# Attention with a mixture of experts on one core: eight multiplies on VectorE, expert adds and fetches later in the pair, outputs through SyncE

## The chip, the cores and the metric

The kernel runs on one core of a Trainium2 chip. A core has four engines that compute, each with an instruction queue of its own that it works off in order: TensorE (PE: matrix products, results go to the banks of PSUM), VectorE (DVE), ScalarE (ACT) and GpSimd (POOL). SyncE (SP) only issues transfers. Transfers (DMAs) are issued from the queues of SP, ACT or POOL. An instruction that has to wait, for another engine or for a transfer, holds everything behind it on its queue.

The metric is the time of one execution on the device in microseconds (us). The profile is of one execution, taken by the hardware profiler; its times are in us from its start.

## The reference, cut to what matters

The input x is 8 sequences of 512 tokens with 256 channels. The result is x plus attention plus a feed-forward layer, both of the normalised x.

```python
x = L0_attn_x                                   # (8, 512, 256)
xn = layernorm(x)
# attention: 16 heads of 64, keys and values through a latent of 128
latent = xn @ w_kv_down
k, v = split(latent @ w_kv_up); q = xn @ w_q
att = softmax(causal(q k^T / 8)); y = att v     # per head
attn = y @ w_out
# feed-forward: each token goes to its top 2 of 8 experts, and through shared weights
scores = sigmoid(xn @ gate_w.T + lb_bias); topw, topi = top_k(scores, 2)
topw = topw / (topw.sum(-1) + 1e-8)
for e in range(8):
    sel = (topi == e).any(-1); wmean = mean of topw over the tokens of e
    out = out + where(sel, mlp_e(xn) * wmean, 0)
out = out + shared_mlp(xn)
return x + attn + out
```

All of it is in float32.

## The kernel before, in words

**Pairs.** The work is laid out over 64 pairs of heads, m = 8 b + p for sequence b and pair p (line 813). For a pair, `scores` makes the products of q and k in four row blocks on TensorE; VectorE adds the mask and takes the minimum (L662), ScalarE takes the exponential and its sums (L669), VectorE transposes the result in blocks of 32 into the tile `blk` (`transposed`, L682 and L689). `moved` (L701) brings `blk` to `pt` with 16 transfers of 80 KB, so that keys lie on the partitions; in most pairs GpSimd issues 5 of them and SP 11. `inverse_sums` takes the reciprocal of the sums (L718), transposes it (L721), and sends it to a row in DRAM (GpSimd's queue, L723). `spread_sums` loads that row, broadcast over partitions, as `rb` (SP's queue, L731). Two pairs later (LAG = 2) `weighted` multiplies v and `pt` on TensorE into the PSUM bank `ps_y` (L744), ScalarE copies it to the tile `yT` (L756) and GpSimd multiplies `yT` by `rb` (L757). With `by_vector`, which only the last two pairs use, VectorE makes one product of `ps_y` and `rb` (L754).

**Projection.** Two to three pairs after a sequence's last head pair, `project` multiplies all its `yT` and the shared experts' hidden values with the output weights (`ps_o`, L118), ScalarE copies the result (L780), and `add_projection` adds it to the sums `acc_d` in DRAM with an accumulating transfer from GpSimd's queue (L786). `acc_d` began as a copy of x.

**Experts.** After the router, each token's normalised row is scattered to two slots in DRAM (`xg_d`, sorted by expert) with indirect transfers of 128 rows from GpSimd (`scatter`, L478, two for each of 32 tiles, and 14 for empty slots). This fills pairs S0 = 14 to 21. In these pairs GpSimd issues one `pt` transfer instead of five and ScalarE up to five. From pair E0 = BLOCK0 = 22 on, 39 tiles of 256 slots pass through the experts. For tile t: `expert_fetch` gathers the expert's weights (GpSimd, L517) and loads the rows `xg` (SP, L524); `expert_turn` transposes them on TensorE (`ps_x`) and copies their token numbers (`to`, GpSimd, L544); `expert_hidden` and `expert_down` make the products, and ScalarE writes `ye` (L569); `expert_add` adds `ye` to the rows of `acc_d`, with an indirect accumulating transfer of 128 rows from GpSimd (L576), two for each tile. Since any of these may touch any row of `acc_d`, each of them waits until the write to `acc_d` before it has landed.

**Order of the work.** All engines' queues are in the order in which the program is written out. `put(m, place, f)` enters a step in the plan of pair m (L808), and each pair's steps are issued by rising place; steps of one place in the order of entry. Up to pair 21 a pair has two halves (places from 0 and from 1), each with a group of scores; `moved` and `inverse_sums` for a pair are issued in the next pair, and `weighted` stands at place 1.4. From pair 22 on a pair has one block of scores. There the multiplication `weighted` of two pairs before comes first, and `inverse_sums` and `moved` of the pair itself are issued ahead of the first step whose place is above HALF:

```python
EARLY, HALF = 0.3, 0.65
...
if place > HALF and chunks:
    while chunks:
        transposed(*chunks.pop(0))
    inverse_sums(*pairs[m])
    moved(*pairs[m], 8 if m >= END else 5)
f(*a)
```

`put_half(h, place, f)` enters a step in half h, that is pair h // 2 at h % 2 + place. With it, tile t has its own half h (L925), from 49 on in steps of one or two. Its fetch stands five halves before, its two adds two and three halves after. So the places of fetches are 0.5 and 1.5, and those of adds 0.45 and 1.45. `rb` of the pair before is loaded at 0.34, the projection's steps stand at 0.75 and 1.7.

**The end.** From pair END = 59 on `bring_out` copies the finished sums of seven sequences from `acc_d` to the output (L792, from ScalarE's queue), one per half, places 0.7 and 1.7. The last sequence's sums are loaded, added to its projection on VectorE (L775) and stored by SP.

Of the kernel before, what the change touches and what calls it, by code (L numbers as in the profile page):

```python
# [33 lines left out]
F32 = mybir.dt.float32  # L34
# [7 lines left out]
P = 128  # L42
# [7 lines left out]
def kernel(  # L50
# [17 lines left out]
    nc = tc.nc  # L68

    B, T, C = x.shape  # L70
# [18 lines left out]
    NU = SLOTS // P  # L89
# [21 lines left out]
    def bank(shape, name):  # L111

        return psum.tile(shape, F32, tag="w", name=name)

    def product(out, lhsT, rhs, start, stop):

        for j in range(2):
            nc.tensor.matmul(  # L118
                out[ts(j, D)], lhsT[:, ts(j, D)], rhs, start=start, stop=stop
            )  # L120

    xf = x.rearrange("b t c -> (b t) c")
    outf = out.rearrange("b t c -> (b t) c")
# [99 lines left out]
    acc_d = dram.tile([NT_ALL, C], F32, name="acc_d")  # L223
# [337 lines left out]
    def expert_down(t):  # L561
        w = fetched[t][0]
        ps = bank([P, NU, C], "ps_ed")
        for u in range(NU):
            product(
                ps[:, u, :], hidden[t][:, ts(u, P)], w[:, ds(WD, C)], start=True, stop=True
            )
        y = ep.tile([P, NU, C], F32, bufs=3, name="ye")
        nc.scalar.mul(y, ps, coef[:, t : t + 1])  # L569
        results[t] = y  # L570

# [122 lines left out]
    def moved(b, p, by_pool, by_act=0):  # L694


        pt = ptp.tile([P, NB, 2, NBLK, QB], F32, name="pt")

        def begin(by, k):
            a, kb = divmod(k, NB)  # L700
            by.dma_start(pt[ts(kb, QB), a], blks[b, p][ts(a, QB), kb])  # L701

        left = []
        for k in range(NB * NB):
            if k * by_pool % 16 < by_pool:
                begin(nc.gpsimd, k)
            elif k % 3 == 1 and len(left) < by_act:
                left.append(k)
            else:
                begin(nc.sync, k)  # L710
        pts[b, p] = pt
        return lambda: [begin(nc.scalar, k) for k in left]

    def inverse_sums(b, p):


        ri, riT = ris[p % len(ris)]
        nc.vector.reciprocal(  # L718
            ri[:, : 2 * NQ], rss[b, p].rearrange("p j i -> p (j i)")
        )  # L720
        nc.vector.transpose(riT, ri)  # L721
        row = rowp.tile([NB, QB, QB], F32, name="row")
        nc.gpsimd.dma_start(row.rearrange("a x q -> (a x) q"), riT)  # L723
        rows[b, p] = row
# [64 lines left out]
        )  # L789

    def bring_out(b):
        nc.scalar.dma_start(outf[ts(b, T), :], acc_d[ts(b, T), :])  # L792

    def bring_back():
        nc.sync.dma_start(
# [8 lines left out]
    S0 = 14  # L804
# [3 lines left out]
    def put(m, place, f, *a):  # L808
        if place >= 2:
            m, place = m + 1, place - 2  # L810
        plan.setdefault(m, []).append((place, len(plan[m]) if m in plan else 0, f, a))

    pairs = [(b, p) for b in range(B) for p in range(NPAIR)]
    LAG = 2
    products = {}
    for m, (b, p) in enumerate(pairs):
        if m + 1 < len(pairs):
            put(m, 0.22, keys, *pairs[m + 1])
            put(m, 0.24, queries, *pairs[m + 1])
        if m < BLOCK0 - 1:  # L820
            put(m + 1, 0.32, inverse_sums, b, p)
        put(m + 1, 1.32 if m + 1 < BLOCK0 else 0.34, spread_sums, b, p)
        if m + LAG < BLOCK0:
            put(m + LAG, 1.4, weighted, b, p)
        else:
            products[m + LAG] = (b, p)
        put(m, 1.25 if m < BLOCK0 else 0.26, values, b, p * 2 // VH, p % 2)
    for b in range(B):
        m = b * NPAIR
# [39 lines left out]
    def put_half(h, place, f, *a):  # L869
        put(h // 2, h % 2 + place, f, *a)  # L870
# [5 lines left out]
    for b in range(1, B):  # L876
        h = (b - 1) * LNH // 2
# [41 lines left out]
        xouts = ep.tile([P, NQ, C], F32, name="xout")  # L919

    END = len(pairs) - 5
    put(E0, 0.1, begin_experts)
    first, n_halves = 2 * E0 + 5, 2 * (END - E0) - 7
    for t in range(NET):
        h = first + t * n_halves // NET  # L925
        put_half(h - 5, 0.5, expert_fetch, t)
        put(h // 2, -1, expert_turn, t)
        put(h // 2, (0.23, 0.67)[h % 2], expert_hidden, t)
        put_half(h + 1, 0.15, expert_down, t)
        for u in range(NU):  # L930
            put_half(h + 2 + u, 0.45, expert_add, t, u)
    for b in range(B - 1):
        put_half(2 * END + b, 0.7, bring_out, b)
    put_half(2 * END + B - 1, 0.7, bring_back)

# [3 lines left out]
    for m in range(len(pairs) + 1):  # L939
# [48 lines left out]
        for place, _, f, a in todo + [(2, 0, lambda: None, ())]:  # L988
# [3 lines left out]
# [6 lines that stand above are left out]
# [59 lines left out]
```

## Time and profile before

| | |
|---|---|
| time, median of 3 runs | 936.95 us (930.66 to 940.15) |
| profiled execution, own time | 937.93 us |
| its span, first to last instruction | 936.2 us |
| mean granted TensorE clock | 0.98 |
| TensorE busy | 888.7 us (95%) |
| GpSimd busy | 602.7 us (64%) |
| VectorE busy | 580.5 us (62%) |
| ScalarE busy | 506.7 us (54%) |
| scatters L478 | 62.6 us for the 64 of token rows, 979 ns each |
| multiplies of yT L757 on GpSimd | 88.2 us, 62 |
| indirect adds L576 | 127.5 us, 78, 1635 ns each |

How to read it: a group's row names line, engine, operation and the tiles it writes and reads; "L757 POOL TENSOR_TENSOR yT<-yT,rb 128x512" is GpSimd multiplying `yT` by `rb`. Busy time is the time in which instructions compute, or in which GpSimd makes up the descriptors of a transfer. Waiting and SP's or ACT's issuing of transfers are not busy. For a transfer, the duration at its line is that of its issue, and the data lands later. In a list of waits, the engine and the line that waited are named first, then what ended the wait; where it waited for several things, the name is that of the last one. "PEclk" is the share of TensorE's full clock that was granted.

### The profile page before, as it was taken

To read this page: it belongs to the slowest core of one execution; us is meant where nothing else is said; L and a number is where in the kernel's file an instruction comes from. 1 tells how busy PE (TensorE), PEld (TensorE's weight loads), DVE (VectorE), ACT (ScalarE), POOL (GpSimd) and SP (SyncE) were. 2 spreads that over 40 slices of the span, in tenths; PEclk is the share of its full clock that TensorE was granted. 3 is DMA by queue.
4 is the path that set the end of the run, shared out by engine and by line. 5 is a ranking of instruction groups with operands and counts; after the bars stand their busy time and mean duration, and the time that the engine had idled before them with its cause. 6 is when DMAs were issued, how large, how long until landed. Compare 5 with 4: busy or idle time off the path is not lost. (4 is left out here: it accounts for less than half of the span.)

```text
span 936.2 us, 20693 instructions
## 1 busy us (share of the span) xinstructions
PE 888.7 (95%) x6564; PEld 471.2 (50%) x6564; DVE 580.5 (62%) x2049; ACT 506.7 (54%) x1520; POOL 602.7 (64%) x840
## 2 busy tenths in 40 slices
PE   7897999988699899999999999899999999989898
PEld 3343555333354455645555545565556654546446
DVE  3887766996345785376753767535676356763761
ACT  3665565445335475465754666545576456753550
POOL 2795782388888855648676566675667656767460
PEclk9899999999999999999999999999999999999999
DMA  7578787468768898778888788887788687866782
GB/s 242 137 210 215 210 251 191 105 184 274 244 200 230 259 239 206 172 164 195 204 184 195 175 191 196 189 199 166 176 197 216 154 196 167 209 144 160 201 249 76
DMA packets 125195, 181.87 MB, mean 194 GB/s; under 512 B 24704, under 2 KB 88448, under 8 KB 124848
## 3 DMA queue, kind: packets, MB, share of 16 engines
q1 hardware_dynamic: 87760, 104.06, 39.8%
q0 software_dynamic: 34624, 69.28, 32.7%
q10 hardware_dynamic: 2704, 7.22, 2.6%
q8 instruction: 53, 0.87, 0.4%
q14 instruction: 54, 0.44, 0.2%
HBM read 66.45 MB, written 41.14 MB: 115 GB/s over the span
## 5 line engine op out<-in xcount | busy, mean ns | idle before, releaser
L662 DVE CUSTOM_DVE_ANT_0 ps_s<-ps_s,mask 128x128 f32<-128x128 f32 (+3 forms) x512 | 238.9, 519 | 189.2 <-PE ps_s L655 186.2
L669 ACT ACTIVATE pr<-ps_s,mn 128x128 f32<-128x128 f32 (+3 forms) x512 | 269.0, 537 | 125.0 <-DVE mn L662 94.5
L682 DVE STREAM_TRANSPOSE blk<-pr 128x384 f32<-128x384 f32 (+2 forms) x512 | 207.1, 446 | 33.4 <-ACT pr L669 16.3
L576 POOL DMA_INDIRECT acc_d<-ye,to x78 | 127.5, 1635 | 133.3 <-DMA acc_d<-ye,to 61.8
L701 POOL DMA_DIRECT2D pt<-blk x303 | 164.2, 692 | 42.9 <-DVE riT L721 22.3
L744 PE MATMUL ps_y<-pt,v 128*64 128x512 f32 (+3 forms) x1024 | 159.0, 454 | 21.6 <-DMA rb<-row 11.0
L655 PE MATMUL ps_s<-k,q 64*128 64x128 f32 (+3 forms) x1024 | 169.5, 449 | 9.5 <-ACT pr L669 4.5
L655 PEld LDWEIGHTS ps_s<-k,q 64*128 64x128 f32 x1024 | 92.3, 188 | 71.7 <-issue 36.7
L118 PE MATMUL ps_o<-wo_sb,yT 128*64 128x256 f32 x1024 | 121.1, 380 | 6.3 <-POOL yT L757 6.3
L744 PEld LDWEIGHTS ps_y<-pt,v 128*64 128x64 f32 x1024 | 75.0, 141 | 103.1 <-issue 73.7
L118 PE MATMUL ps_q<-xnT,wq_sb 128*64 128x512 f32 x512 | 122.9, 601 | 0.0
L757 POOL TENSOR_TENSOR yT<-yT,rb 128x512 f32<-128x512 f32 x62 | 88.2, 1423 | 50.7 <-ACT yT L756 32.9
L669 ACT ACTIVATION_READ_ACCUMULATOR pr<-ps_s,mn 128x1 f32 x512 | 108.3, 212 | 0.0
L118 PEld LDWEIGHTS ps_o<-wo_sb,yT 128*64 128x64 f32 x1024 | 77.3, 137 | 40.5 <-POOL yT L757 6.8
L118 PE MATMUL ps_e<-xgT,w 128*64 128x256 f32 x624 | 74.1, 379 | 0.0
L662 DVE DVE_READ_ACCUMULATOR2_ANT mn<- 128x1 f32 x512 | 72.5, 142 | 0.0
L118 PEld LDWEIGHTS ps_q<-xnT,wq_sb 128*64 128x64 f32 x512 | 38.3, 140 | 67.7 <-issue 60.0
L478 POOL DMA_INDIRECT xg_d<-xn,at_i x64 | 62.6, 979 | 13.3 <-issue 11.8
L118 PE MATMUL ps_k<-lat,wkv_sb 128*64 128x512 f32 x256 | 69.7, 622 | 1.0 <-ACT lat L600 1.0
L118 PE MATMUL ps_v<-wkv_sb,lat 128*64 128x256 f32 x512 | 68.4, 387 | 0.0
L780 ACT COPY po<-ps_o 128x256 f32<-128x256 f32 x28 | 10.4, 372 | 106.6 <-PE ps_o L118 106.6
L756 ACT COPY yT<-ps_y 128x512 f32<-128x512 f32 x62 | 36.6, 590 | 44.8 <-PE ps_y L744 43.4
(141 smaller groups left out, 959.6 us busy)
## 6 DMA issues: line engine op xcount, KB each, us to landing
pt<-blk SPq DMA_DIRECT2D x681, 80.0 KB
pt<-blk POOLq DMA_DIRECT2D x303, 80.0 KB
rb<-row SPq DMA_DIRECT2D x128, 128.0 KB
xg<-xg_d SPq DMA_DIRECT2D x39, 272.0 KB
acc_d<-in_x_dram SPq DMA_DIRECT2D x8, 512.0 KB
xin<-in_x_dram SPq DMA_DIRECT2D x7, 512.0 KB
xnT_d<-lnT SPq DMA_DIRECT2D x7, 512.0 KB
xnT<-xnT_d SPq DMA_DIRECT2D x7, 512.0 KB
```

The source lines that it names most:

```text
L118: nc.tensor.matmul(out[ts(j, D)], lhsT[:, ts(j, D)], rhs, start=start, stop=stop)
L478: ins = nc.gpsimd.indirect_dma_start(out=xg_d[:, :], out_offset=bass.IndirectOffsetOnAxis(ap=at, axis=0), in_=rows, in_offset=None,)
L576: nc.gpsimd.indirect_dma_start(out=acc_d[:, :], out_offset=bass.IndirectOffsetOnAxis(ap=turned[t][1][:, u : u + 1], axis=0), in_=results[t ...
L655: nc.tensor.matmul(pss[j][:, ds(at, n)], q[ts(j, D), ts(i, P)], k[ts(j, D), :n], start=True, stop=True,)
L662: nc.vector.tensor_tensor_reduce(out=pss[j][:, ds(at, n)], in0=pss[j][:, ds(at, n)], in1=mask[:, T - n :], scale=1.0, scalar=NO_MIN, op0=A ...
L669: nc.scalar.activation(o, s, AF.Exp, bias=mn, scale=-1.0, accum_out=rs[:, j, i : i + 1])
L682: nc.vector.transpose(blk[:, :, j, i : i + (nr - 1) * (NQ - 1) + 1 : NQ - 1, :].rearrange("p b c q -> p c b q"), pr[:, j, : nr * P].rearra ...
L701: by.dma_start(pt[ts(kb, QB), a], blks[b, p][ts(a, QB), kb])
L744: nc.tensor.matmul(ps[ts(j, D), :, c:, :], vs[b, h // VH][:, c, ts(h % VH, D)], pts[b, p][:, :, j, at : at + NQ - c, :], start=(c == 0), s ...
L756: nc.scalar.copy(y, ps)
L757: nc.gpsimd.tensor_tensor(y, y, rb, ALU.mult)
L780: nc.scalar.copy(pos[b][:, tt % 2, :], ps)
```

## The change

Three parts.

In pairs 14 to 21, while rows are scattered, `weighted` is called with `by_vector`: VectorE multiplies `ps_y` by `rb` into `yT`, in place of ScalarE's copy and GpSimd's multiply.

From pair 22 on the places of fetches and adds become 0.7 in a pair's first half and 1.45 in its second. 0.7 is above HALF, so `inverse_sums` and `moved` of the pair are issued ahead of them. `expert_fetch` moves as a whole: its gather of weights on GpSimd's queue and its load of rows on SP's. The tile `ye` has five buffers, not three.

`bring_out` issues from SP's queue.

```diff
-        y = ep.tile([P, NU, C], F32, bufs=3, name="ye")
+        y = ep.tile([P, NU, C], F32, bufs=5, name="ye")
...
     def bring_out(b):
-        nc.scalar.dma_start(outf[ts(b, T), :], acc_d[ts(b, T), :])
+        nc.sync.dma_start(outf[ts(b, T), :], acc_d[ts(b, T), :])
...
         if m + LAG < BLOCK0:
-            put(m + LAG, 1.4, weighted, b, p)
+            put(m + LAG, 1.4, weighted, b, p, S0 <= m + LAG)
...
+    def behind(h):
+
+        return h // 2, (0.7, 1.45)[h % 2]
+
     put(E0, 0.1, begin_experts)
     first, n_halves = 2 * E0 + 5, 2 * (END - E0) - 7
     for t in range(NET):
         h = first + t * n_halves // NET
-        put_half(h - 5, 0.5, expert_fetch, t)
+        put(*behind(h - 5), expert_fetch, t)
         put(h // 2, -1, expert_turn, t)
         put(h // 2, (0.23, 0.67)[h % 2], expert_hidden, t)
         put_half(h + 1, 0.15, expert_down, t)
         for u in range(NU):
-            put_half(h + 2 + u, 0.45, expert_add, t, u)
+            put(*behind(h + 2 + u), expert_add, t, u)
```

## The prediction

> **What bounds the kernel now.** I began with the page: engines' shares and the 40 slices.
>
> ```profile
> PE 888.7 (95%) x6564; PEld 471.2 (50%) x6564; DVE 580.5 (62%) x2049; ACT 506.7 (54%) x1520; POOL 602.7 (64%) x840
> ...
> PE   7897999988699899999999999899999999989898
> ```
>
> TensorE looks like the bound, GpSimd (POOL) like an engine with a third to spare. That average misleads, so I took busy times of stretches: 187-323 is about the scatter stage (pairs 14 to 21), 415-860 the expert stage with its adds, and two short ones lie around the worst hole. The columns are busy times of TensorE, its weight loads, VectorE, ScalarE and GpSimd, then the granted clock.
>
> ```profile
> core 0: us, PE busy (x) PEld busy (x) DVE busy (x) ACT busy (x) POOL busy (x), PEclk, DMA share, GB/s
> 187.00:323.00 136.00, 119.32 (x706) 55.26 (x706) 83.15 (x299) 64.59 (x200) 115.41 (x197) 0.95 0.79 232
> 243.00:256.00 13.00, 6.67 (x51) 3.35 (x51) 2.83 (x10) 4.04 (x13) 11.25 (x21) 0.96 0.74 230
> 256.00:269.00 13.00, 13.00 (x84) 6.78 (x84) 4.06 (x17) 3.97 (x12) 11.30 (x21) 0.77 0.74 215
> 415.00:860.00 445.00, 437.69 (x3360) 241.85 (x3358) 272.58 (x940) 260.15 (x774) 294.58 (x353) 0.99 0.79 185
> ```
>
> In the scatter stage TensorE is idle 16.7 us and its clock is below full. The timeline there (start, duration, idle before and who ended it) shows the one long wait:
>
> ```profile
> 254.61 1.28 POOL L757 TENSOR_TENSOR yT<-yT,rb 128x512 f32<-128x512 f32 x1
> ...
> 255.94 1.12 PE L118 MATMUL ps_o<-wo_sb,yT 128*64 128x256 f32 x4 [6.33 <-POOL yT L757]
> ```
>
> The product of that multiply had been copied out of PSUM by ScalarE at 243.9. It stood 10.7 us in GpSimd's queue behind scatters.
>
> In the expert stage I asked what GpSimd itself waits for (total, times, longest):
>
> ```profile
> POOL acc_d L576 <- DMA acc_d<-ye,to: 55.4, 24, 5.1
> POOL acc_d L576 <- issue: 35.6, 32, 4.5
> POOL acc_d L786 <- DMA acc_d<-ye,to: 12.1, 6, 3.1
> POOL acc_d L576 <- ACT xgT L540: 10.4, 3, 6.3
> ```
>
> All rows of that answer that stand before an accumulation into acc_d (L576, L786) add up to 136.7 us, the others to 11.8. With 294.6 busy this makes 443.1 of the 445 us: **GpSimd's queue is full in this stage.** The names "issue" and "ACT xgT" are the last event, not the cause: the adds' operand (ye) was written 10 to 20 us earlier. Each add waits for the landing of the previous write to acc_d. Two neighbours show the price:
>
> ```profile
> 589.44 1.69 POOL L576 DMA_INDIRECT acc_d<-ye,to  x1 [0.30 <-issue]
> 596.25 1.58 POOL L576 DMA_INDIRECT acc_d<-ye,to  x1 [5.13 <-DMA acc_d<-ye,to]
> ...
> 601.88 1.21 POOL L723 DMA_DIRECT2D row<-riT  x1
> ```
>
> The thirteen pairs of accumulations with nothing between them idle 2.88 to 6.29 us, 4.1 on average. The last line is pair 41's row of inverse sums, ready since 589: GpSimd is 13 us late. What that does to TensorE stands in the chain of waits:
>
> ```profile
> 824.15 1.62 DMA acc_d<-ye,to
> 825.77 2.86 issue
> ...
> 829.83 1.17 POOL row L723
> 831.00 1.47 POOL pt L701 x3
> 832.47 2.55 DMA pt<-blk
> ...
> 835.36 4.02 PE ps_y L744 x16
> ```
>
> TensorE lost 3.8 us in the slices of this piece. In 415-860 it lost 7.3 in all.
>
> **The change, part by part,** against the profiled execution: span 936.2, own time 937.9, 1.0 above the median of 936.95.
>
> *Multiply on VectorE, in pairs 14 to 21 (for the heads of pairs 12 to 19).* Gone: 8 GpSimd multiplies at 1.28 plus 0.17 gap, 11.6 us of a queue busy 115 of 136, and 8 ScalarE copies at 0.59, 4.7 us. New: 8 VectorE multiplies out of PSUM at 0.69 (the L754 row has two, at the tail), 5.5 us. The 6.33 us wait goes, since no product stands behind scatters any more. After it TensorE ran at 0.77 of its clock for 13 us: 3.0 us more. In 208-243 ScalarE is in steady work or issuing moves, and 0.59 less per pair may come through for three of them; I take 1.5. Sum: 10.8 us gained. Next late there is ScalarE itself, which issues five pt moves a pair and sat 29.3 us behind them in this stage, so I count no more. For the new wait: VectorE now stands at ps_y and at the rb load, and behind it are the next pair's minima (L662), which ScalarE's exponentials wait for. ps_y of pair 14 ends at 227.6, the minima before it ended at 225.7 and the transposes fill the time till then; the next minima began at 228.05 and then waited 2.36 us for TensorE. That wait covers 0.69, so I cost it at nothing; uncovered it is 5.5 us. The rb loads were issued 3 to 15 us before their ps_y, and come sooner when row stands behind less. Bounds of this part: 5 to 13 gained.
>
> *Adds and fetches behind row and pt.* The instructions are the same; what changes is what stands between two writes to acc_d. GpSimd's order in a pair was: index copy, multiply, add, fetch, row, five pt moves, add, fetch. It becomes: index copy, multiply, row, pt, add, fetch, add, fetch. Ahead of TensorE's needs come row and pt, so the wait shown in the chain is taken off that piece. But row and pt (0.6 + 2.5 us) no longer cover the landing of the pair's first add. I wrote out the plan for pairs 25 to 58: 86 accumulations, 85 intervals.
> Before: 13 with nothing between, 6 with a fetch (1.3 us), 12 with copy and multiply (1.65), 5 with a copy more (1.85), 15 with these and a fetch (2.98), 20 with row and pt (3.15), 14 others. At 4.1 us of idle time less what stands between, this leaves 53 + 17 + 29 + 11 + 17 + 19 + 3 = 149 us. The profile's own waits in 340-900 are 151, so the price holds.
> After: 25 with nothing, 19 with a fetch, 8 with row and pt, 8 with copy and multiply and the like, 25 covered. 102 + 53 + 8 + 15 = 178: **29 us more on a queue that is full.**
> Here a rule of the Trainium skill would turn the sum. "DMA: Bandwidth & Descriptors", Anatomy of one DMA, gives a DMA about 2.0 us fixed plus bytes by 436 GB/s, so 2.3 us for 128 KB (an estimate from the page). At 2.3 the adds' waits would be 47 before and 79 after; the queue would have 100 us of slack and 32 more would be hidden. The row says 4.1, and 149 against 151 confirms it. I follow the row.
> What of 29 reaches the end? GpSimd may fall behind until TensorE waits: row of pair 58 is 8.6 us late now; in pairs of 11.2 us TensorE stalls from about 11 to 12 (pair 56: 12.2 late, stalled 3.8), in longer pairs from about 16. So some 7 us is absorbed, and 22 remain. The stall comes at ps_y (row and pt late in short pairs, as reciprocal, row and everything wait for the former pair's adds) and at the projection, which needs the last pair's yT. Bounds: 0 if the landing gets as quick as the page says, 36 if nothing is absorbed and two or three stalls cost 3 us of clock each, as the hole at 250 did.
>
> *xg loads on SP* move behind the pt moves too. Later tiles have two or three pairs. The first tile has not: its load was issued at 322.9, and with eleven or twelve moves at 0.65 ahead it comes at about 330.6, while its transposes ran at 332.4. Landing takes 3 to 5.7 us here: 1 to 4 lost, I take 2. The buffers of ye (3 to 5) only keep ScalarE from waiting on late adds: 0.
>
> *Outputs through SP.* Seven issues of 0.5 to 0.6 us leave ScalarE and go behind pt of pairs 59 to 62 on SP, ahead of the next rb (868.69, 887.18, 897.82) and pt. SP needed 8.0 to 10.0 us for eight moves there, and ended 0.1 to 0.4 before rb, so two issues delay rb and the next pt by about 1.1. They also wait for the last adds, some 10 us later than now; pairs of 16.7 us hide most of that. ScalarE's exponentials gain the issues. "Issuing engines are not separate DMA queues" in the same page says that only issue time changes hands, as all run on the same 16 engines; by it this part is 0, by the SP rows 1.1 to 2.2 on the late chain. I take 1 lost, between a gain of 2 and a loss of 5.
>
> Sum: 937.9 - 10.8 + 22 + 2 + 1 = 952.1, and 951.1 by the median. I say 951.
>
> **The rivals.**
> *Faster: the queue catches up.* If landing falls to 3 us or less when adds follow adds (the shortest seen was 2.88 idle), the extra waits fit in the slack that this opens, and row and pt being first takes away the 7.3 us of stalls with 1.8 of clock. 937.9 - 10.8 - 9.1 + 3 - 1 = 920. For it speaks the chain; against it the mean of 4.1. It decides where the extra waits stay below the queue's slack. 0.18.
> *A draw.* Half of the extra wait shows (the measured landings go down to 3 in parts, lag absorbed early), 13 against 11: 938 to 940. 0.12.
> *Slower still.* SP waits at rb for late rows, pt and xg behind it come late, the transposes of the expert rows stall, and each stall brings a clock at 0.77: 22 becomes 40, so 969. 0.10.
> *Forecast:* 942 to 963, 0.60.
>
> **How the numbers follow.** About 1% tells no change for this kernel (its three runs span 930.7 to 940.2), so 927.6 to 946.3. Of the forecast's 0.60 a sixth lies below 946. Slower 0.50 + 0.10 = 0.60; same 0.10 + 0.12 + 0.01 = 0.23; faster 0.17. The range reaches from 926, above the heart of the faster case, to 968.
>
> **What would show it.** Right: no wait of ps_o for yT near 250, and clocks of 0.9 or more there; GpSimd's waits before L576 and L786 near 180 us, adds back to back; TensorE waiting 20 us or more at ps_y or ps_o in 415-870, for pt, row or yT; row still 10 to 15 us behind its reciprocal. Wrong: rows within 2 us of the reciprocal throughout, TensorE full in the expert stage. Then the price of a landing was mine to lose. If VectorE waits at L754 for rb by more than 5 us, the first part is wrong.

## The result, and the profile after

| | before | after |
|---|---|---|
| time, median of 20 runs each | 936.11 us (926.90 to 945.06) | 945.75 us (940.13 to 954.63) |
| after / before | | 1.0123, 95% interval 1.0093 to 1.0153 |
| profiled execution, own time | 937.93 us | 954.63 us |
| its span | 936.2 us | 952.9 us |

The medians are of all executions; the ratios, here and below, leave out those more than 1.5% above the fastest of their kernel.

The change costs 9.6 us by the medians, where 14 was forecast. The profiled execution of after is the longest of its runs, 8.9 us above their median; its 16.7 us of added span are therefore more than the change usually costs, and where the other 7 us lie isn't known, so the sizes below are rough. I place the difference with one event in each pair of heads, the start of VectorE's reciprocal (L718):

| from, to | before | after | difference | forecast |
|---|---|---|---|---|
| start to reciprocal of pair 13 | 202.1 | 202.9 | +0.8 | 0 |
| scatter stage, to pair 22 | 120.1 | 113.5 | -6.6 | -10.8 |
| expert stage, to pair 59 | 537.9 | 559.8 | +21.9 | +24 (adds 22, xg 2) |
| tail, to the end | 76.1 | 76.7 | +0.6 | +1 |

The page of after, engines' shares and TensorE's slices:

```profile
PE 894.5 (94%) x6564; PEld 470.4 (49%) x6564; DVE 585.2 (61%) x2057; ACT 502.4 (53%) x1512; POOL 590.2 (62%) x832
...
PE   8997999988998899999999998999969999989798
```

Again the shares say little: GpSimd is less busy than before, and it is GpSimd that costs the time. The windows of after, same stretches and columns as before:

```profile
187.00:323.00 136.00, 125.88 (x750) 56.71 (x748) 92.81 (x325) 64.80 (x205) 110.82 (x197) 0.96 0.82 241
243.00:256.00 13.00, 11.81 (x76) 5.54 (x76) 6.67 (x26) 5.38 (x17) 10.96 (x21) 1.00 0.87 264
256.00:269.00 13.00, 13.00 (x106) 7.16 (x104) 5.90 (x20) 6.35 (x20) 11.17 (x21) 1.00 0.89 269
415.00:860.00 445.00, 424.05 (x3236) 235.30 (x3234) 264.03 (x910) 252.46 (x748) 274.28 (x333) 0.98 0.75 179
```

The hole near 250 is gone (TensorE 11.81 of 13 us where it had 6.67), and the clock behind it is full where it was 0.77. In the expert stage TensorE is idle 20.95 us where it was 7.31. GpSimd's own waits there, in after (total, times, longest):

```profile
POOL acc_d L576 <- DMA acc_d<-ye,to: 72.6, 24, 6.0
POOL acc_d L576 <- ACT pr L669: 20.7, 5, 4.6
POOL acc_d L576 <- DMA pt<-blk: 17.2, 6, 5.3
```

From 340 us to about pair 62's reciprocal, all waits ahead of an accumulation add up to 181.2 us, against 151.1 before. The hand count of intervals gave 178 against 149. Accumulations with nothing between them are 25 in after, as counted, and 13 before; they idle 4.2 us on average, as before (4.1). GpSimd's timeline in after shows both kinds of neighbours:

```profile
463.03 1.60 POOL L576 DMA_INDIRECT acc_d<-ye,to  x1 [2.87 <-ACT xgT L540]
...
465.42 1.20 POOL L723 DMA_DIRECT2D row<-riT  x1
466.03 3.09 POOL L701 DMA_DIRECT2D pt<-blk  x5
470.06 1.68 POOL L576 DMA_INDIRECT acc_d<-ye,to  x1 [0.94 <-DMA acc_d<-ye,to]
476.27 1.60 POOL L576 DMA_INDIRECT acc_d<-ye,to  x1 [4.53 <-DMA acc_d<-ye,to]
```

The add at 470.06 has row and pt ahead of it and waits 0.94; the one at 476.27 follows an add directly and waits 4.53. The change makes more of the second kind. Rows fall further behind their reciprocals: 13.3 us on average in pairs 33 to 48, up to 18.8, against 8.1 before. TensorE's waits, first before and then after, from 320 us to the end:

```profile
PE ps_y L744 <- DMA pt<-blk: 3.8, 1, 3.8
PE ps_y L744 <- DMA rb<-row: 3.6, 2, 2.6
PE ps_y L744 <- ACT pr L669: 2.5, 1, 2.5
PE ps_y L744 <- DMA xg<-xg_d: 1.8, 1, 1.8
PE ps_y L744 <- DMA row<-riT: 1.3, 2, 0.8
```

```profile
PE ps_y L744 <- DMA pt<-blk: 13.8, 4, 7.4
PE ps_x L534 <- DMA xg<-xg_d: 6.6, 3, 4.5
PE ps_y L744 <- DMA rb<-row: 4.8, 1, 4.8
PE ps_y L744 <- ACT pr L669: 2.9, 3, 1.6
PE ps_e L118 <- DMA w<-wall_d,wrow_i: 2.2, 2, 1.6
PE ps_o L118 <- POOL yT L757: 0.5, 1, 0.5
```

These are 13.0 us before and 30.8 after. In the expert stage itself, without 3.9 and 4.8 us that lie in the tail (its waits for rb and row), they are 9.1 and 26.0. Of these 16.9 us more, 7.6 are at ps_y, 8.8 at the late fetches (xg and w) and 0.5 at ps_o. The other 5.0 of the 21.9 us are longer busy time for the same matmuls, and that goes with the clock: it was granted at half for 20.5 us of this stage, in three stretches around the long waits at 330, 714 and 838, where before had two of 3.4 us.

### The profile page after: what moved, and what is told of

It is laid out like the page before. It is cut to its first block, busy times and chain, and to the rows that moved or that the text cites. A ratio compares the mean times of both kernels' runs of the same rounds, so it can differ in the third digit from the quotient of the medians.

```text
span 952.9 us, 20647 instructions
## 1 busy us (share of the span) xinstructions
PE 894.5 (94%) x6564; PEld 470.4 (49%) x6564; DVE 585.2 (61%) x2057; ACT 502.4 (53%) x1512; POOL 590.2 (62%) x832
## 4 chain that ended last, share of the span: by engine, by line
PE 58%; DMA 21%; SPq 7%; DVE 5%; POOL 4%; issue 3%; ACT 2%; ACTq 0%; POOLq 0%; DVEq 0%
PE ps_o L118 13%; PE ps_y L744 10%; DMA pt<-blk 8%; PE ps_s L655 8%; PE ps_q L118 7%; SPq L701 5%; PE ps_e L118 5%; PE ps_k L118 4%; PE ps_gu L118 4%; DMA row<-riT 4%; PE ps_v L118 3%; DMA rb<-row 3%; DMA acc_d<-ye,to 2%; PE ps_ed L118 2%; DMA xg<-xg_d 2%
## 5 line engine op out<-in xcount | busy, mean ns | idle before, releaser
L701 POOL DMA_DIRECT2D pt<-blk x303 | 163.9, 695 | 38.8 <-DVE riT L721 10.4
L655 PE MATMUL ps_s<-k,q 64*128 64x128 f32 (+3 forms) x1024 | 172.1, 452 | 9.3 <-ACT pr L669 3.1
L757 POOL TENSOR_TENSOR yT<-yT,rb 128x512 f32<-128x512 f32 x54 | 79.3, 1469 | 45.8 <-ACT yT L756 29.1
L118 PEld LDWEIGHTS ps_o<-wo_sb,yT 128*64 128x64 f32 x1024 | 74.8, 137 | 37.0 <-issue 1.7
L723 POOL DMA_DIRECT2D row<-riT x64 | 49.5, 774 | 24.6 <-DVE riT L721 15.8
L756 ACT COPY yT<-ps_y 128x512 f32<-128x512 f32 x54 | 31.9, 590 | 58.5 <-PE ps_y L744 57.5
```

The lines of the kernel that those rows point to most:

```text
L118: nc.tensor.matmul(out[ts(j, D)], lhsT[:, ts(j, D)], rhs, start=start, stop=stop)
L655: nc.tensor.matmul(pss[j][:, ds(at, n)], q[ts(j, D), ts(i, P)], k[ts(j, D), :n], start=True, stop=True,)
L756: nc.scalar.copy(y, ps)
L757: nc.gpsimd.tensor_tensor(y, y, rb, ALU.mult)
```

## The experiments

They ran on two chips: the first four together on one, the other eight on a second, four at a time. The kernel before took 947.80, 955.71 and 954.55 us beside them, not 936, so every ratio below is to the kernel before on the same chip. Which chip the comparison above ran on isn't recorded; its two profiles are called the first pair below. There is no profile of the kernel before on the two chips: `e3_outputs`, which differs from it behind pair 59 only, stands in for it. The lengths of stages are from one profiled execution each.

### One part at a time

`e1_multiply`, the kernel before with the first part alone:

```diff
-            put(m + LAG, 1.4, weighted, b, p)
+            put(m + LAG, 1.4, weighted, b, p, S0 <= m + LAG)
```

> The first part alone: in pairs 14 to 21 VectorE multiplies yT, all else as before. Queue theory (the loss is in GpSimd's order of adds): 6 to 11 us faster than before, no wait of TensorE for yT near 250, VectorE's wait at L754 covered. Rival (VectorE standing at ps_y holds the minima and is what cost time): no gain or 3 to 6 us slower.

`e2_late`, the kernel before with `behind` for fetches and adds and with five `ye` buffers:

```diff
-        put_half(h - 5, 0.5, expert_fetch, t)
+        put(*behind(h - 5), expert_fetch, t)
...
-            put_half(h + 2 + u, 0.45, expert_add, t, u)
+            put(*behind(h + 2 + u), expert_add, t, u)
```

> The second part alone: fetches and adds behind row and pt, ye with five buffers, multiply and outputs as before. Queue theory: 16 to 22 us slower than before, waits in front of the accumulations on GpSimd about 180 us, row of inverse sums 10 to 18 us behind its reciprocal in pairs 41 to 58. Rival (the loss is in SP's queue at the end): within 3 us of before.

`e3_outputs`, the kernel before with the outputs on SP:

```diff
-        nc.scalar.dma_start(outf[ts(b, T), :], acc_d[ts(b, T), :])
+        nc.sync.dma_start(outf[ts(b, T), :], acc_d[ts(b, T), :])
```

> The third part alone: outputs through SP. Queue theory: within 2 us of before. Rival (outputs ahead of rb and pt on SP make the end late): 4 to 10 us slower, and the last four pairs longer by that.

`e4_multiply_outputs` has the edits of e1 and e3.

> First and third part without the late adds. Queue theory: 6 to 11 us faster than before, the same as the first part alone within 2 us. Rival (outputs on SP cost): 4 us or more slower than the first part alone.

| | median | ratio to before (95%) | scatter stage | expert stage | tail |
|---|---|---|---|---|---|
| e1_multiply | 969.95 | 1.0231 (1.0167 to 1.0295) | 164.3 | 533.1 | 74.3 |
| e2_late | 968.11 | 1.0243 (1.0183 to 1.0302) | 130.7 | 548.7 | 78.1 |
| e3_outputs | 943.88 | 0.9963 (0.9924 to 1.0003) | 131.7 | 538.1 | 72.8 |
| e4_multiply_outputs | 969.89 | 1.0240 (1.0178 to 1.0303) | 163.5 | 530.3 | 71.6 |

The late adds cost 20 us by the medians, as expected. Their profile is of the shortest execution, 7 us under its median, and shows 16 of them: 10.6 us in the expert stage and 5.3 in the tail, beside e3. The waits ahead of accumulations are 167 us there (180 was expected) against 142 in e3, rows 12 us late in pairs 41 to 58. The outputs alone gained 3.9 us by the medians, outside the 2 expected, but the interval reaches nothing, and e4 is as long as e1. The multiply is a plain miss: 22 us lost where 6 to 11 gained was expected, twice. The stage lengths put the loss where the multiply is: 164 us of scatter stage against 131 with GpSimd's multiply on the same chip. TensorE sat idle 46.5 us of it where it was 20.0, and its clock was 0.82, not 0.95. The waits of e1 from 203 to 366 us name it:

```profile
ACT pr L669 <- DVE mn L662: 40.1, 7, 9.9
DVE yT L754 <- remote: 30.7, 3, 10.7
...
PE ps_s L655 <- DVE yT L754: 20.3, 2, 10.3
```

VectorE stood three times for about 10 us at L754, and behind it ScalarE (no minima) and TensorE (no free bank). That is the standing which the prediction costed at nothing and put at 5.5 us uncovered. "remote" says that the view found no event of this core to end the wait.

### The adds: does the wait for the former write make the loss?

`e5_two_sums_late` is the changed kernel with the second add of each tile going to another tile in DRAM, so that two neighbours don't wait for each other. Half of the experts' results is thereby left out of the output. The second sum also begins as a copy of x: eight more transfers, 4.2 MB, most of them in the scatter stage.

```diff
-            out=acc_d[:, :],
+            out=(acc_d, acc2_d)[u][:, :],
```

> The changed kernel, but the second add of each tile goes to a second tensor in DRAM that also begins as a copy of x and never reaches the output (so half of the experts' adds are left out of the result). It takes away half of the waits for the landing of the write before, with the order of the queue kept. Queue theory: GpSimd catches up, row within 6 us of its reciprocal in most pairs of the expert stage, TensorE's stalls there under 5 us, and 920 to 932 in all. Rival (xg, rows and outputs late on SP): 940 or more, and TensorE still waits for pt and xg.

`e6_two_sums` has the same edit on e4, that is with the old order of adds and fetches; the same half is left out.

> The same second tensor (half of the experts' adds left out of the result) in the old order of fetches and adds, with the first and third part. Queue theory: when waiting for the landing is no longer the bound, order is worth little: 920 to 932, within 4 us of the same edit in the new order. Rival: 10 us or more faster than in the new order.

The other way to relieve GpSimd is to take its multiplies away in the expert stage too. `e7_late_all_vector` does it to the changed kernel, `e8_all_vector` to e4:

```diff
-            weighted(*products.pop(m))
+            weighted(*products.pop(m), True)
```

> The changed kernel, and VectorE multiplies yT in the expert stage too: 1.45 us a pair (about 50 in all) off GpSimd's queue, 0.69 a pair onto VectorE's. Queue theory: that is more than the 29 us that the new order put on it, so the stalls go: 918 to 932. Rival (GpSimd's work is not what counts, the landing chain of 86 adds alone is): 940 or more, rows still 10 us late.

> First and third part, adds in the old order, and VectorE multiplies yT in the expert stage too. Queue theory: GpSimd gets slack in the old order, 915 to 926, and the old order's stalls at 585, 700 and 830 go. Rival (VectorE standing at ps_y delays transposes and minima): slower than with the multiply in the scatter stage alone.

| | median | ratio to before (95%) | scatter stage | expert stage | row behind reciprocal, pairs 33 to 48 |
|---|---|---|---|---|---|
| e5_two_sums_late | 972.75 | 1.0160 (1.0091 to 1.0229) | 159.3 | 532.8 | 1.2 us |
| e6_two_sums | 964.78 | 1.0089 (1.0061 to 1.0118) | 165.5 | 526.8 | 1.3 us |
| e7_late_all_vector | 976.86 | 1.0208 (1.0140 to 1.0276) | 156.9 | 542.6 | 8.8 us |
| e8_all_vector | 976.16 | 1.0200 (1.0128 to 1.0273) | 171.5 | 530.3 | 8.0 us |

All four totals missed: 915 to 932 us was expected. All four carry VectorE's multiply in the scatter stage, and its loss on these chips hides in every total, so only the expert stage can be read. The groups of the page for the indirect adds, first of the changed kernel repeated on e5's chip (`e10_after_again`, below) and then of e5:

```profile
L576 POOL DMA_INDIRECT acc_d<-ye,to x78 | 126.7, 1625 | 164.6 <-DMA acc_d<-ye,to 88.9
```

```profile
L579 POOL DMA_INDIRECT acc_d<-ye,to x78 | 126.7, 1624 | 29.5 <-issue 21.1
```

With two sums the idle time ahead of the adds falls from 164.6 to 29.5 us, rows follow within 1.2 us on average, and the stage with late adds becomes 20 us shorter (553.0 in e10 to 532.8). The stage of e10 is no odd one: in e11, e12 and e13 below, which leave it as it is, it takes 549.7, 550.8 and 557.0. With the old order the second sum makes it 3.5 us shorter (e4 to e6, which ran on different chips). So the waits for the former write make some 17 us of what the late order costs, between 11 and 21 with these other stages and with e1's 533.1 for e4's. 6 us remain between the two orders without these waits (e6 to e5), and TensorE's waits in e5 show where (8.0 us in this stage, where under 5 was expected; the second row lies in the tail):

```profile
PE ps_x L537 <- DMA xg<-xg_d: 7.2, 2, 6.9
PE ps_y L747 <- DMA pt<-blk: 2.1, 1, 2.1
```

e6 has no wait for xg at all. It is the first tile's rows, loaded behind the pt moves: TensorE waited 4.5 us for them in after, 5.7 in e2, 6.9 here.

Taking the multiplies from GpSimd gave 7 to 14 us of this stage in the late order (550 to 557 in the four profiles, 542.6 in e7), and nothing in the old one (530.3 in e4 and e8, on different chips). Rows stayed 8 to 9 us behind in both. Some 50 us of multiplies became waiting: from pair 22 to pair 62, all waits ahead of accumulations rose from 146.7 (e4) to 197.2 us (e8), and in the late order from 173.6 (e10) to 203.2 (e7). So in the old order nearly all of GpSimd's multiplies, and in the late one about half, lay in time in which it would have waited for a landing anyway.

### The scatters: what holds VectorE at L754?

In the semaphore events of e1, L754 waits for TensorE alone. The matmuls of its ps_y are recorded at 239.06 to 241.38, but TensorE's count reaches the others at 251.35, three steps within 0.1 us, and it is so again in the pairs around it. Such late counts (more than 2 us behind the last end that is recorded before them, so the figures are least values) stand in the scatter stage of each of the eight kernels above, up to 5.4 us in e2 and e3, where GpSimd multiplies, and 8.1 to 11.1 us in the six others. In the two profiles of the first pair there is none above 0.4 us. And it is TensorE alone: the counts of VectorE, ScalarE and GpSimd, as far as they are recorded, are never over 1.1 us behind in this stage, in any profile. Four more runs were to say what makes them. `e10_after_again` is the changed kernel itself.

> The changed kernel itself, beside the variants of it below and on their chip. Theory (the multiply on VectorE loses where TensorE's completions are seen late while rows are scattered, and that belongs to the chip and not to one of the three parts): the scatter stage (reciprocal of pair 13 to that of pair 22) takes 155 to 165 us as in every run so far that had VectorE's multiply there, and the three parts add up: +22 for the multiply, +20 for the late adds, -4 for the outputs, 38 us in 950, a ratio of about 1.04. Rival (the parts don't add up, the late adds take the multiply's loss away): the stage takes about 114 us as in the profile of the changed kernel, and the ratio is about 1.012.

In `e11_gate` GpSimd has to wait for VectorE's product as it once had to wait for ScalarE's copy:

```diff
         if by_vector:
             nc.vector.tensor_tensor(y, ps, rb, ALU.mult)
...
+        if seen:
+            nc.gpsimd.tensor_copy(between, yT[:, 0:1])
...
-            put(m + LAG, 1.4, weighted, b, p, S0 <= m + LAG)
+            put(m + LAG, 1.4, weighted, b, p, S0 <= m + LAG, S0 <= m + LAG)
```

> The changed kernel, and GpSimd copies one column of y^T behind each multiply of the scatter stage, so that it waits for the product as it did when it multiplied itself. Theory (GpSimd's own wait at the multiply broke its run of scatters, and without it the run delays TensorE's completions): the scatter stage is 25 to 30 us shorter than in the repeat of the changed kernel, 125 to 135 us, if that repeat shows about 160. Rival (what counts is that VectorE stands in front of the minima until ps_y is seen complete; GpSimd's pacing is nothing): the stage is as long as the repeat's within 5 us, or longer by the 0.3 us of the copy and its wait per pair.

`e12_plain` leaves the sorting by expert out:

```diff
+    placed = iter(range(NET * SLOTS // P))
...
-        ins = nc.gpsimd.indirect_dma_start(
-            out=xg_d[:, :],
-            out_offset=bass.IndirectOffsetOnAxis(ap=at, axis=0),
-            in_=rows,
-            in_offset=None,
-        )
+        ins = nc.gpsimd.dma_start(xg_d[ts(next(placed), P), :], rows)
```

> The changed kernel with each scatter replaced by a plain write of the same 128 rows by GpSimd to a fixed place; the sorting of rows by expert is left out, so each expert tile works on other rows. Theory (it is the scatter by index that delays what others see of TensorE): TensorE's late completions go, VectorE waits under 1 us at the multiply, and the scatter stage takes 105 to 115 us. Rival (the delay comes with the load of the transfers, whatever their form, or from TensorE itself): the stage is as long as the repeat's within 10 us, with waits of 5 to 10 us at the multiply.

`e13_later` takes VectorE away from ps_y, with `multiply` at place 0.3 of the next pair:

```diff
+    def multiply(b, p):
...
+        nc.vector.tensor_tensor(y, y, rb, ALU.mult)
...
-            nc.gpsimd.tensor_tensor(y, y, rb, ALU.mult)
+            if not later:
+                nc.gpsimd.tensor_tensor(y, y, rb, ALU.mult)
...
+            if S0 <= m + LAG:
+                put(m + LAG + 1, 0.3, multiply, b, p)
```

> The changed kernel, but in the scatter stage ScalarE copies ps_y out as before and VectorE multiplies that copy in the next pair, behind the minima of its first group, so that VectorE never stands at ps_y. Theory (it is VectorE's place in front of the minima that hands the late completion on): the scatter stage takes 125 to 132 us, what GpSimd's multiply gave on such a chip, or up to 6 us less. Rival (late completions hold the minima through ps_s all the same, and the cause is GpSimd's unbroken run of scatters): 155 to 165 us, as in the repeat of the changed kernel.

| | median | ratio to before (95%) | scatter stage | most scatters in a row | latest count of TensorE |
|---|---|---|---|---|---|
| e10_after_again | 998.72 | 1.0300 (1.0206 to 1.0395) | 166.8 | 9 | 10.4 us |
| e11_gate | 984.02 | 1.0286 (1.0231 to 1.0342) | 152.6 | 7 (9 in its first pair) | 7.9 us (6.1 behind its first pair) |
| e12_plain | 950.09 | 0.9956 (0.9929 to 0.9984) | 117.2 | none by index | none above 0.4 us |
| e13_later | 993.95 | 1.0401 (1.0350 to 1.0452) | 159.6 | 9 | 8.6 us |
| e3_outputs, from above | 943.88 | 0.9963 (0.9924 to 1.0003) | 131.7 | 7 | 5.4 us |
| after, first pair | 945.75 | 1.0123 (1.0093 to 1.0153) | 113.5 | 9 | none above 0.4 us |

The six executions of e10 lie between 978 and 1006 us; its ratio is of the two shortest, its profile of one of 997 us. The eight profiles with runs of nine (e1, e4 to e8, e10, e13) are the better measure of such a stage: 156.9 to 171.5 us.

e10 answers first: the loss comes with where, or under what conditions, the kernel runs, not with one part meeting another. The same program took 113.5 us for this stage in the first pair and 166.8 here, and lost 3% in all. The sum of the parts, 1.04, is just above its interval. e10's timeline shows one hold:

```profile
237.21 2.32 PE L744 MATMUL ps_y<-pt,v 128*64 128x512 f32 x16
...
247.13 0.97 POOL L478 DMA_INDIRECT xg_d<-xn,at_i  x1 [0.19 <-issue]
250.31 0.69 DVE L754 TENSOR_TENSOR yT<-ps_y,rb 128x512 f32<-128x512 f32 x1 [10.99 <-remote]
...
251.05 2.08 PE L655 MATMUL ps_s<-k,q 64*128 64x512 f32 x4 [11.09 <-DVE yT L754]
251.35 0.37 ACT L669 ACTIVATE pr<-ps_s,mn 128x128 f32<-128x128 f32 x1 [8.60 <-DVE mn L662]
```

The product ends at 239.53 by its records. From 236.85 to 248.10 GpSimd issues nine scatters with nothing between but a fill of one column (L486, 0.11 us) behind each, as in every kernel here, and VectorE sees the product at 250.31, 2.2 us after the last of them was issued. TensorE's next scores wait 11 us for VectorE.

e12 says that the scatters by index are at the root. With plain writes of the same rows, not one count was late, VectorE never waited over 3 us at the multiply, and the stage took 117.2 us (105 to 115 was expected), not 166.8. Load alone is not the cause. The windows of the scatter stage, e10 and then e12 (columns as above, GB/s last):

```profile
199.10:365.90 166.80, 120.61 (x648) 52.92 (x646) 72.76 (x257) 54.28 (x172) 94.29 (x168) 0.85 0.62 173
203.20:320.40 117.20, 107.25 (x634) 49.03 (x632) 73.14 (x258) 52.59 (x171) 57.13 (x168) 0.93 0.82 246
```

e12 moved 246 GB/s on average, against 173 of e10 over its own stage. It can't tell whether it is the writing by index or the time that GpSimd takes to issue it, 0.54 us a piece here against 0.97, because both changed.

e11 was between its two expectations: its stage is 14 us shorter than e10's, where the theory said 25 to 30 and the rival at most 5. It is also 4 us shorter than the shortest of the other eight. The totals don't show it: 1.0286 and 1.0300. Its timeline of GpSimd and of VectorE's product:

```profile
245.82 0.96 POOL L478 DMA_INDIRECT xg_d<-xn,at_i  x1 [0.19 <-issue]
249.54 0.18 POOL L759 COPY between<-yT 128x1 f32<-128x1 f32 x1 [2.64 <-DVE yT L754]
251.68 0.98 POOL L478 DMA_INDIRECT xg_d<-xn,at_i  x1 [1.96 <-issue]
```

```profile
248.71 0.69 DVE L754 TENSOR_TENSOR yT<-ps_y,rb 128x512 f32<-128x512 f32 x1 [6.62 <-remote]
```

Seven scatters end at 246.8, and VectorE's product came at 248.71 after 6.62 us of standing, not 11. In the old form, the multiply L757 stood at this place, and broke the run in seven and two. In e11's first pair the copy found the product done and held nothing up, so that nine went out almost in a row, and there stands its latest count, 7.9 us; behind it none is over 6.1. So the length of the run seems to matter, on one profile of e11, and it is not all.

e13 says that VectorE's place at ps_y is not what makes the loss: without it the stage, 159.6 us, is within the range of those with it, and the ratio is no better. The minima are held in its stead. Its waits from 201 to 361 us:

```profile
DVE ps_s L662 <- PE ps_s L655: 31.0, 7, 14.8
...
DVE ps_s L662 <- remote: 27.7, 6, 11.0
```

What follows: on the experiments' chips VectorE's multiply loses time because what TensorE has finished is seen late while scatters by index are issued, and e12 shows that it takes these scatters. GpSimd, once it has no multiply of its own, sends them in runs of nine, and e11 suggests that a shorter run holds the others for less. Why 21 us still lie between e11 and e3, where runs are of seven too, stays open (they ran on different chips); e3 has ScalarE waiting at ps_y and GpSimd's 1.28 us of multiply in the run, e11 has VectorE there. Open as well is why the first pair shows no late count in the same program. And the records can't tell whether TensorE's count travels late or its matmuls end later than they are recorded; that the other three engines' counts are on time speaks for something in TensorE.

One rival is left untested, that the recording of the profile has part in it. Of the 72 to 80 steps of GpSimd's count in the scatter stage, the profiles of before, after and e12 hold all, and the eleven others lack 54 to 63. So in this stage GpSimd's records are lost in just those profiles in which TensorE's counts are late. It is not the whole story: in the expert stage all twelve experiments, e12 too, lack 63 to 98 of TensorE's some 564 steps (15 in before, 8 in after), and no count there is over 1.3 us late.

## Why the prediction was right or wrong

**Slower, and by about that much: right.** 951 was 5.3 us above the measured median, and the loss of 9.6 us was sized at 14. 945.75 lies just inside what the prediction counted as no change (to 946.3), but the interval of the ratio lies clear of 1. That the number came so close owes something to luck. It is a sum of terms of both signs, the gain was sized too high in it and one term of the loss too, and on the second chip the same kernels differ by 3%, some 29 us (e10).

**The price of neighbouring adds: right.** 29 us more of waiting, by counting what stands between two writes to acc_d at 4.1 us a landing; measured 30.1 (181.2 less 151.1), and the 25 direct neighbours that were counted are there. The trace's row was the right one to follow: with landings at the 2.3 us estimated from the Trainium skill ("DMA: Bandwidth & Descriptors", Anatomy of one DMA), the late order would have cost nothing in the sum, and it cost 20 us by itself (e2). The rivals that rested on quick landings, at 0.18 and 0.12, fall with it.

**What of it reaches the end: right in sum, mixed in its parts.** 22 plus 2 for xg were forecast, 21.9 measured in the profiled execution. But the term for xg was too small: the first tile's load cost TensorE 4.5 us, not 2. It was issued at 324.4 behind eleven moves, as forecast, but TensorE had it only 6.2 us later, where 3 to 5.7 were allowed. Later tiles, counted at nothing, waited another 2.1 for rows and 2.2 for weights. So the adds' share is nearer 13 to 17 than 22: 17 is what the experiments give to their waits (20 less 3.5), and in after 13 of the 21.9 are left when 8.8 is taken off for the fetches. 5 of these 13 go with the clock, which the prediction left out of the 22 and put in its bound only. Of the 29 us, 12 to 16 were absorbed, not 7.

**The multiply: the mechanism that was named is right, the sum isn't.** The 6.33 us wait of ps_o for yT is gone, and the clock behind it is full. But the stage gained 6.6, not 10.8. The step that failed is "I cost it at nothing", the standing of VectorE at L754. In after it waited for rb once:

```profile
244.21 0.69 DVE L754 TENSOR_TENSOR yT<-ps_y,rb 128x512 f32<-128x512 f32 x1 [2.53 <-DMA rb<-row]
```

TensorE's scores waited 2.5 us in all for that multiply in this stage. This leaves 8.3 of the forecast 10.8; the other 1.7 is not placed. On the experiments' chips the term has the other sign, +22 us (e1): VectorE stood there not for rb but for TensorE's late count, which the trace of before doesn't show, so it could not be foreseen from it. The bounds "5 to 13 gained" were thus too sure. They were drawn from one profile, and a stage 33 us longer (e1 beside e3) was outside them.

**The outputs: small, as forecast, with the sign open.** The tail is 0.6 longer where 1 was forecast, which is too little to tell. Alone they gave 0.9963 (0.9924 to 1.0003), between 7 us gained and nothing, so the gain of 2 that bounded this term was set too low.

**The forecast of what the profile would show: right but for one size.** No wait of ps_o near 250, clock full there; waits ahead of the accumulations of 181 where "near 180" was said; rows 13 us late on average in pairs 33 to 48. TensorE's waits at ps_y in 415-870 are 16.7 us (the first and fourth row of its answer), not 20 or more; the rest of its time was lost at the fetches.

## What to carry to other kernels

When each of a queue's instructions waits for the landing of the one before it, count the intervals between them by what fills them, at the landing that the trace shows: useful work that is moved out from between two of them costs that queue as much as it had covered, and what the queue's lag can't absorb reaches the end (here 13 to 17 of 29 us). Work that is taken off such a queue may only turn into waiting, as the multiplies did in e8. An instruction that is taken off a queue also closes a gap there, so ask what the work that now runs in one piece does to the others. A term of a few us that rests on one profile may have the other sign elsewhere, as the multiply's did on two other occasions here.

## What the runs showed of the hardware

With GpSimd's scatters by index going out in a row, others saw TensorE's results up to 11.1 us after their recorded ends, on two chips, in all the kernels that had such scatters there: up to 5.4 us where GpSimd multiplied between them, and 7.9 to 11.1 us where VectorE did. The recorded counts of the other engines were not over 1.1 us late. With plain writes in place of them, no count was late by 2 us on the second of these chips (e12). The first pair of profiles, taken where the kernel before is 12 to 20 us shorter, show none with the same instructions. And of the 165 us that GpSimd sat idle ahead of accumulating transfers, two sums took 135 away, but only 20 us of the stage.
